# A division on VectorE queued one planner slot earlier, and the transposes of its result placed behind a mask product

## Chip, cores, metric

One Trainium2 chip (trn2), one NeuronCore of it. The metric is the device time of one launch in microseconds (us). Engines are called as the profile calls them: PE (TensorE; PEld is its weight load), DVE (VectorE), ACT (ScalarE), POOL (GpSimd), SP (SyncE, which issues most DMAs). PSUM is the memory that PE writes its products to; a "bank" is one 128 x 512 float32 tile of it.

## What is computed

Two transformer layers over x of shape (4, 512, 256), float32 throughout:

```python
x = x + L0_attn(layernorm(x))   # 16 heads of 16, causal softmax, output projection
x = x + L0_ffn(layernorm(x))    # per output unit: softmax over 8 experts, top 2, weighted expert outputs
x = x + L1_attn(layernorm(x))   # 16 query heads of 128, 4 kv heads, over groups of 4 rows
x = x + L1_ffn(layernorm(x))    # gate/up/down with 4-bit weights, gelu
```

The change lies in the first line, where the attention's mixed values are divided by the sums of the powers:

```python
att = jax.nn.softmax(jnp.where(causal, -1e9, q @ k.T / 4), axis=-1)
out = att @ v                       # (b, h, q, d)
return out.transpose(0, 2, 1, 3).reshape(b, s, d) @ w_out.T
```

## The kernel before

**Tiling.** Rows lie as 4 blocks j of 4 sequences s with 128 rows each. The first layer's attention runs over 44 batches n (line 810). A batch is a block, a sequence and some of the four groups g of four heads: 4 groups at a time in block 0 (4 batches, n = 0 to 3), 2 in block 1 (n = 4 to 11), 1 in blocks 2 and 3 (n = 12 to 27 and 28 to 43). So 16 times, once for each (j, s), the groups of a sequence are complete and are divided.

**One batch.** The program writes out the order of PE, DVE and POOL by hand (manual_schedule, line 69): these engines run in the order of the Python text. ACT's and SP's orders in this part are left to the scheduler, which is told to put the batch's own work first (high_priority). For batch n the text issues:

1. greatest(n+1): PE scores s1 into four banks of the pool l0_sc, which has five (L631).
2. shift(n): PE transposes batch n's row maxima (mxT, L660), DVE subtracts them from the queries (qk, L663).
3. mask(n+1): PE adds the causal mask (L644), DVE takes the row maxima of the four tiles (mx, L650).
4. a **first slot** (fill, line 826).
5. mixed(n-1): PE multiplies powers with values (av, L715), ACT copies the result to SBUF (avs, L723).
6. powers(n): PE scores again, transposed (s, L679, four banks of l0_sc), ACT takes exponentials (pt, L688), POOL masks them (L698).
7. a **second slot** (line 834), ahead of which divided() of a completed sequence is put at the head of the streams.

**Slots.** fill() counts the variable slot up by one, gives PE and DVE a budget of some us, and lets the streams (generators) emit pieces in order of the list while budget is left. A piece names its engine, a planned cost and a least number of slots since the stream's last piece. Pieces are the next block's projections (qk_ps L529, v_ps L551), bias folds (a product L244 and two DVE additions to rw or ew, L250), layernorms, the router's and the experts' products (lg_ps, eo, L226) and the DVE work that turns router logits into weights (L363 to L420). The left-over of the budget decides which piece comes in which slot, so that a piece moved by one slot moves later pieces too. Slots 1, 3, 5, ... are first slots as long as no extra fill is made between blocks.

**The two banks.** Every product that a slot's pieces make goes into a tile of the pool dn, which has two banks (line 97). A bank is free again when ACT (copy) or DVE has read it. The tile of the transposed mixed values (av_T), that of the transposed divided values (oq_T) and all pieces' tiles share these two banks.

**divided(j, s)** (lines 727 to 773), three steps: four PE transposes of avs into av_T (L733); on DVE a reciprocal of the sums (rden, L739) and a product (oq, L740), which are av_T's readers; two PE transposes of oq into oq_T (L748), which ACT copies to aT (L751). After the last sequence of a block, the output projection (o, L760) and the addition to x (L770) follow, and a stream for the next layernorm is added. Each step waits one slot after the one before: with av_T in the second slot of batch n, the division comes in the first slot of batch n+1, behind mask(n+2) on DVE, and oq_T in the second slot of n+1, behind powers(n+1) on PE and, in ACT's order, behind its four exponentials.

**After it.** From about 432 us on the second layer's attention runs (its weights wqkv are loaded then), with what is left of the router and expert products between its own; then the second FFN, nearly PE alone. The stage tile (one buffer, lines 581 and 539) holds projected queries and keys until eight DMAs have moved them to qk.

Of the kernel before, what the change touches and what calls it, by code (L numbers as in the profile page):

```python
# [32 lines left out]
def tile_transformer(  # L33
# [75 lines left out]
    slot = 0  # L109

    def need(engine, cost, gap=0, cond=None):
        return engine, cost, gap, cond
# [25 lines left out]
    left = {"PE": 0.0, "DVE": 0.0}  # L138
# [117 lines left out]
    def hidden_pieces(b):  # L256

        out = []
        done = (4 * b - 5, 1)
        last = b == NBLK - 1  # L260
        yield from norm_pieces(b, b1, b2, out, cond=lambda: b < 2 or done in halves)
        xT = b2.tile([P, 2, 512], F32, tag="xT", name=f"xT{b}")
        for hc in range(2):
            yield need("PE", 0.5, 0 if hc else 1 + last)
            ps = transposed(out[0], hc, ps_dn, "dn", f"xT_ps{b}_{hc}")
            ps = ps.rearrange("p t q -> p (t q)")
            if hc:
                nc.scalar.activation(xT[:, hc, :], ps, AF.Identity, bias=last_16)
            else:
                nc.scalar.copy(xT[:, hc, :], ps)  # L270
        normed.clear()
        xTs[b] = xT
# [160 lines left out]
    with ExitStack() as l0:  # L433
# [293 lines left out]
        def divided(j, s):  # L727

            yield need("PE", 0.5, 1)
            avs = avs_of.pop((j, s))  # L730
            ps = ps_dn.tile([P, NH0, 32], F32, tag="dn", name=f"av_T{j}_{s}")
            for g in range(4):
                nc.tensor.transpose(  # L733
                    ps[:, 4 * g : 4 * g + 4].rearrange("p h d -> p (h d)"), avs[:, g], ident
                )
            rden = a2.tile([P, NH0], F32, tag="rden", name=f"rden_{j}_{s}")
            oq = a1.tile([P, NH0, 16], F32, tag="oq", name=f"oq_{j}_{s}")
            yield need("DVE", 0.7, 1)
            nc.vector.reciprocal(rden, ps[:, :, 16])  # L739
            nc.vector.tensor_tensor(  # L740
                oq, ps[:, :, 0:16], rden.unsqueeze(2).to_broadcast([P, NH0, 16]), ALU.mult
            )
            yield need("PE", 0.3, 1)
            if not s:
                aTs[j] = a1.tile([P, 2, 16, NS, 8], F32, tag="aT", name=f"aT{j}")
            ps = ps_dn.tile([P, 2, P], F32, tag="dn", name=f"oq_T{j}_{s}")
            for k in range(2):
                nc.tensor.transpose(  # L748
                    ps[:, k], oq[:, 8 * k : 8 * k + 8].rearrange("p h d -> p (h d)"), ident
                )  # L750
            nc.scalar.copy(aTs[j][:, :, :, s, :], ps.rearrange("p k (g b) -> p k g b", b=8))  # L751
            if s < NS - 1:
                return

            for t in (0, 2):
                yield need("PE", 1.75, 1 if j or not t else 0)
                ps = ps_dn.tile([P, 2, HID], F32, tag="dn", name=f"o0_{j}_{t}")
                for i in range(2):
                    for k in range(2):
                        nc.tensor.matmul(  # L760
                            ps[:, i],
                            lhsT=aTs[j][:, k, 4 * (t + i) : 4 * (t + i) + 4].rearrange(
                                "p g s b -> p (g s b)"
                            ),
                            rhs=wo[:, k, :], start=k == 0, stop=k == 1,
                        )
                if j:
                    yield need("DVE", 0.7, 1)
                both = xres[:, 4 * j + t : 4 * j + t + 2, :]
                nc.vector.tensor_tensor(both, both, ps, ALU.add)  # L770
            fold_at = streams.index(fold) if fold in streams else len(streams) - 4
            streams.insert(fold_at if j else 0, Stream(hidden_pieces(j)))
# [37 lines left out]
        for n in range(NBT):  # L810
# [21 lines left out]
            if n and batches[n - 1][2][-1] == 3:  # L832
                streams.insert(0, Stream(divided(*batches[n - 1][:2])))
# [11 lines left out]
        mixed(NBT - 1)  # L845
        streams.insert(0, Stream(norm_pieces(0, b1, b2, normed_first)))
        last = Stream(divided(*batches[NBT - 1][:2]))
        streams.insert(0, last)
        while last.next is not None:
# [435 lines left out]
```

## Time and profile before

| | us |
|---|---|
| median of 3 runs | 1226.32 (1224.99 to 1227.24) |
| the profiled execution | 1226.09 |
| its span, first to last instruction | 1224.3 |
| PE busy in the span | 1170.2 (96%) |
| DVE busy | 805.4 (66%) |
| ACT busy | 483.7 (40%) |
| POOL busy | 101.4 (8%) |

How to read it: on the page "busy" is the time in which an engine ran an instruction; PEclk is the clock that PE was granted, 1 for full. In a list of waits, "PE fold L244 <- ACT stage L533: 4.1, 4, 2.1" says that PE's product for the tile fold stood idle for 4.1 us in 4 places, 2.1 at most, until ACT's copy to the tile stage ended. In a timeline a row has start, duration, engine, line, operation, tiles written and read, and in brackets the idle time before it with what ended it. A table of stretches has, for each, its length and the busy time of each engine.

### The profile page before, as it was taken

What the parts mean: (1) busy time and instruction counts of PE and PEld (TensorE: products, weight loads), DVE (VectorE), ACT (ScalarE), POOL (GpSimd) and SP (SyncE); (2) the same over time, 40 slices, a digit from 0 to 9 for tenths busy, and PEclk for the clock granted to TensorE, in tenths of its full rate; (3) what the DMA queues carried; (4) which work ended last, traced back from release to release, by engine and by line L of the source; (5) the groups of instructions that cost most, each with busy time, mean ns of one, the idle gap of its engine ahead of it and who ended that gap; (6) DMA issues with size and microseconds to landing.
All of it is one profiled execution on the core that took longest, in us unless ns stands there. A gap on an engine that the chain in (4) does not pass through costs nothing.

```text
span 1224.3 us, 18602 instructions
## 1 busy us (share of the span) xinstructions
PE 1170.2 (96%) x7178; PEld 672.7 (55%) x7178; DVE 805.4 (66%) x1783; ACT 483.7 (40%) x1099; POOL 101.4 (8%) x152
## 2 busy tenths in 40 slices
PE   7879999999989998999999999999999999999998
PEld 4545545455545543555555555656645456475487
DVE  5546658898878848726872886688599963734710
ACT  1423444564545544434443444355344331312300
POOL 7312101111111100000000000000000000000000
PEclk9999999999999999999999999999999999999999
DMA  7321010000000050000000001012020000000000
GB/s 209 68 55 18 2 32 5 1 2 1 1 1 2 1 172 1 1 1 1 1 1 1 1 1 35 16 46 44 1 52 17 1 1 18 0 1 18 0 1 34
DMA packets 21240, 26.46 MB, mean 22 GB/s; under 512 B 5128, under 2 KB 14600, under 8 KB 21152
## 3 DMA queue, kind: packets, MB, share of 16 engines
q1 hardware_dynamic: 20480, 24.10, 7.4%
q10 hardware_dynamic: 672, 1.18, 0.4%
q8 instruction: 56, 0.92, 0.3%
q14 instruction: 32, 0.26, 0.1%
HBM read 18.97 MB, written 2.10 MB: 17 GB/s over the span
## 4 chain that ended last, share of the span: by engine, by line
PE 80%; DVE 13%; ACT 3%; issue 1%; DMA 1%; POOL 1%; SPq 1%; ACTq 0%; DVEq 0%; POOLq 0%
PE qk_ps L965 10%; PE y L1212 9%; PE o L1056 9%; PE g L893 8%; PE u L893 8%; PE lg_ps L226 8%; PE eo L226 7%; PE s L631 5%; DVE mx L650 3%; PE s L679 2%; PE v_ps L947 2%; PE av L715 2%; PE qk_ps L529 2%; PE a L1036 1%; PE s L978 1%
## 5 line engine op out<-in xcount | busy, mean ns | idle before, releaser
L965 PE MATMUL qk_ps<-xT,wqkv 128*128 128x512 f32 x320 | 148.8, 599 | 1.4 <-ACT qT L969 0.8
L226 PE MATMUL lg_ps<-rw,xT 128*128 128x512 f32 x256 | 129.1, 628 | 6.9 <-ACT part L315 2.9
L226 PE MATMUL eo<-ew,xT 128*128 128x512 f32 x256 | 122.1, 600 | 4.9 <-ACT part L315 2.4
L1056 PE MATMUL o<-wpj,oT 128*128 128x256 f32 x512 | 119.6, 382 | 0.0
L1212 PE MATMUL y<-wd,it 128*128 128x256 f32 x512 | 111.8, 379 | 0.0
L1056 PEld LDWEIGHTS o<-wpj,oT 128*128 128x128 f32 x512 | 95.8, 190 | 27.8 <-issue 14.8
L1212 PEld LDWEIGHTS y<-wd,it 128*128 128x128 f32 x512 | 97.0, 190 | 15.0 <-issue 2.2
L650 DVE TENSOR_REDUCE mx<-s 128x1 f32<-128x384 f32 (+3 forms) x176 | 100.3, 631 | 1.3 <-PE s L644 1.3
L965 PEld LDWEIGHTS qk_ps<-xT,wqkv 128*128 128x128 f32 x320 | 59.1, 190 | 70.8 <-issue 57.5
L688 ACT ACTIVATE pt<-s 128x512 f32<-128x512 f32 (+1 forms) x176 | 83.6, 560 | 18.6 <-PE s L679 18.6
L893 PE MATMUL g<-xT,wgu 128*128 128x512 f32 x192 | 90.4, 593 | 0.0
L893 PE MATMUL u<-xT,wgu 128*128 128x512 f32 x192 | 90.2, 592 | 0.0
L315 ACT ACTIVATE part<-eo,c 128x256 f32<-128x256 f32 x128 | 53.8, 473 | 85.9 <-PE eo L226 82.4
L698 POOL TENSOR_SCALAR_AFFINE_SELECT pt<-pt 128x256 f32<-128x256 f32 (+2 forms) x88 | 56.0, 640 | 309.2 <-ACT pt L688 308.5
L226 PEld LDWEIGHTS lg_ps<-rw,xT 128*128 128x128 f32 x256 | 48.1, 199 | 53.5 <-issue 39.5
L1190 ACT ACTIVATE th<-sq 128x512 f32<-128x512 f32 x64 | 40.3, 630 | 87.6 <-DVE sq L1189 87.6
L631 PE MATMUL s<-qk 32*128 32x128 f32 (+3 forms) x512 | 71.0, 485 | 2.5 <-ACT pt L688 2.3
L226 PEld LDWEIGHTS eo<-ew,xT 128*128 128x128 f32 x256 | 46.2, 190 | 48.8 <-issue 36.8
L214 DVE TENSOR_TENSOR xres<-xres,y 128x256 f32<-128x256 f32 x16 | 6.7, 421 | 92.5 <-PE y L1212 92.5
L342 DVE TENSOR_TENSOR part<-part 128x512 f32<-128x512 f32 x32 | 22.1, 691 | 67.1 <-ACT part L315 67.1
L289 ACT COPY lg<-lg_ps 128x512 f32<-128x512 f32 x64 | 37.7, 589 | 71.3 <-PE lg_ps L226 71.1
L177 POOL TENSOR_TENSOR ln_rs<-rs_v,minus_half 128x4 f32<-128x4 f32 x16 | 17.8, 1112 | 555.6 <-DVE rs_v L176 305.3
(233 smaller groups left out, 1788.9 us busy)
## 6 DMA issues: line engine op xcount, KB each, us to landing
qk<-stage SPq DMA_DIRECT2D x56, 64.0 KB, 2.4
wqkv<-in_w_qkv SPq DMA_DIRECT2D x8, 320.0 KB, 6.4
rw<-in_router_w SPq DMA_DIRECT2D x8, 256.0 KB, 7.7
ew<-in_expert_w SPq DMA_DIRECT2D x8, 256.0 KB, 4.3
wpj<-in_w_proj SPq DMA_DIRECT2D x1, 2048.0 KB
out<-xres SPq DMA_DIRECT2D x4, 512.0 KB, 2.6
xres<-in_x SPq DMA_DIRECT2D x3, 512.0 KB, 9.0
dq_wgu<-in_gate_w SPq DMA_DIRECT2D x8, 128.0 KB, 2.4
```

The lines of the kernel that those rows point to most:

```text
L226: nc.tensor.matmul(ps, lhsT=xT[:, hc, (g % 4) * P : (g % 4 + 1) * P], rhs=w[:, hc, 2 * pair : 2 * pair + 2, :].rearrange("p e o -> p (e o) ...
L289: nc.scalar.copy(lg[:, 2 * pair : 2 * pair + 2, :].rearrange("p e o -> p (e o)"), ps)
L315: nc.scalar.mul(part[:, e % 4], ps[:, i], c[:, e : e + 1])
L631: nc.tensor.matmul(tiles[h][:, b * nk : (b + 1) * nk].rearrange("p (c k) -> p c k", k=P), lhsT=queries(j, g)[r, s], rhs=qk[r, g, : j + 1, ...
L650: nc.vector.tensor_reduce(maxes[n % 2][:, h, gs[0] : gs[0] + nb], ps[:, : nb * nk].rearrange("p (b k) -> p b k", b=nb), AX.X, ALU.max,)
L688: nc.scalar.activation(pt[:, i, : nb * nk], tiles[2 * pair + i][:, : nb * nk], AF.Exp, scale=0.25)
L698: nc.gpsimd.affine_select(out=last, in_=last, compare_op=ALU.is_ge, fill=0.0, base=0, pattern=pattern, channel_multiplier=-1,)
L893: nc.tensor.matmul(ps, lhsT=wgu[:, w, half, jj, par * P : (par + 1) * P], rhs=xT[:, half, :], start=half == 0, stop=half == 1,)
L965: nc.tensor.matmul(ps, lhsT=wqkv[:, hc, kv, h, :], rhs=xT[:, hc, :], start=hc == 0, stop=hc == 1,)
L1056: nc.tensor.matmul(ys[t // 2][:, t % 2], lhsT=state["o"][:, h, t * P : (t + 1) * P], rhs=wpj[:, HPK * kv + h, :], start=kv == 0 and h == 0 ...
L1190: nc.scalar.activation(th, sq, AF.Tanh, scale=0.7978845608028654)
L1212: nc.tensor.matmul(ps, lhsT=it[:, c // 2, c % 2, t * P : (t + 1) * P], rhs=wd[:, c // 2, c % 2, :], start=c == 0, stop=c == 2 * NJ - 1,)
```

## The change

The division is no longer a piece of its own: the reciprocal and the product are issued to DVE directly after the four transposes, in the same slot, and their 0.7 us are taken off DVE's budget. The transposes of the divided values are still at least one slot later, but only in a slot with an odd number, which is a first slot, behind mask().

```diff
         yield need("PE", 0.5, 1)
         avs = avs_of.pop((j, s))
...
-            yield need("DVE", 0.7, 1)
+            left["DVE"] -= 0.7
             nc.vector.reciprocal(rden, ps[:, :, 16])
             nc.vector.tensor_tensor(
                 oq, ps[:, :, 0:16], rden.unsqueeze(2).to_broadcast([P, NH0, 16]), ALU.mult
             )
-            yield need("PE", 0.3, 1)
+
+            yield need("PE", 0.3, 1, cond=lambda: slot % 2)
```

In the built programs both kernels hold the same instructions; their order differs from the first division on. The steps of divided() for a sequence then stand so: av_T and the division in the second slot of batch n, oq_T in the first slot of batch n+1 (for one sequence, j = 3 and s = 1, three batches later, since no budget is left in the first slots between).

## Prediction, made before the changed kernel ran

> **What bounds the kernel now.** I read the page first: PE is busy 96% of the span, so the end is set by PE's work and by the 54 us in which PE is idle. Then the table of stretches, cut where the batches of block 0 (to 105.1), block 1's first five (to 144.7), the rest of the first attention (to 432) and the start of the second layer (to 482) end:
>
> ```profile
> core 0: us, PE busy (x) PEld busy (x) DVE busy (x) ACT busy (x) POOL busy (x), PEclk, DMA share, GB/s
> 45.00:105.10 60.10, 47.65 (x473) 29.18 (x473) 31.72 (x58) 19.38 (x38) 13.94 (x17) 0.94 0.25 55
> 105.10:144.70 39.60, 35.53 (x405) 22.47 (x404) 24.30 (x54) 15.95 (x32) 8.36 (x12) 0.96 0.01 1
> 144.70:432.00 287.30, 273.90 (x2730) 149.41 (x2730) 231.51 (x562) 147.44 (x399) 43.45 (x71) 0.97 0.03 5
> 432.00:482.00 50.00, 42.71 (x129) 18.26 (x127) 31.00 (x90) 22.68 (x64) 0.00 (x0) 0.97 0.32 106
> ```
>
> Sixteen of PE's idle us lie in the first 100 us of this, at 0.94 and 0.96 of the clock. DVE is half busy there, 81% later. What PE waits for between 45 and 145, by the list of waits:
>
> ```profile
> PE fold L244 <- ACT stage L533: 4.1, 4, 2.1
> PE qk_ps L529 <- ACT aT L751: 3.6, 2, 2.0
> PE x_ps L202 <- ACT xT L566: 2.3, 2, 1.7
> PE v_ps L551 <- ACT aT L751: 1.7, 1, 1.7
> PE fold L244 <- ACT va L557: 1.3, 2, 0.7
> ```
>
> None of these products reads what it waits for: a fold needs neither stage nor va. They wait for a dn bank. The timeline of batch 2 shows why two banks act as one:
>
> ```profile
> 57.04 0.66 PE L733 MATMUL av_T<-ident,avs 128*128 128x128 f32 x4
> 57.18 2.06 ACT L688 ACTIVATE pt<-s 128x512 f32<-128x512 f32 x4 [0.53 <-PE s L679]
> 57.53 0.38 PE L748 MATMUL oq_T<-ident,oq 128*128 128x128 f32 x2
> ...
> 59.11 0.40 ACT L751 COPY aT<-oq_T 128x256 f32<-128x256 f32 x1
> 59.56 1.99 PE L551 MATMUL v_ps<-wp,xT 128*128 128x256 f32 x8 [1.65 <-ACT aT L751]
> ...
> 62.23 0.38 PE L244 MATMUL fold<-rows 128*128 128x512 bf16 x1 [0.67 <-ACT va L557]
> ...
> 66.78 0.38 PE L244 MATMUL fold<-rows 128*128 128x512 bf16 x1 [0.67 <-ACT va L557]
> 66.98 0.24 DVE L739 RECIPROCAL rden<-av_T 128x16 f32<-128x16 f32 x1
> ```
>
> av_T is written at 57.04, and its reader on DVE comes at 66.98, behind four row maxima: for ten us one bank is out of use. The other goes to oq_T, whose copy stands behind four exponentials (57.18 to 59.24), so v_ps idles 1.65, and each product after it waits for the copy of the one before.
>
> **Part 1: the division moves up.** DVE runs it right behind av_T. In this stretch DVE is idle then (6.33 us ahead of its addition at 62.65), so its 0.67 us (0.24 and 0.42) cost PE nothing, and the bank is free about 0.9 us after av_T, while PE runs the 1.82 us product in the other bank. In the built order that product takes the bank of the last fold, already added, and only the fold after it takes av_T's bank. On DVE the shift is queued behind the division; it waits for mxT, 4 us after av_T. **Part 2: oq_T moves behind the mask**, where ACT has no exponentials ahead of it: its 0.4 us copy is done before the next bank is needed.
>
> **Block 0**, at full clock, PE start to start: av and s 2.12 (54.92 to 57.04), av_T 0.49, a 512-wide product 1.82 (45.41 to 47.23), fold 0.31, s1 with mxT and mask 1.57 (62.54 to 64.11), oq_T 0.27. A new batch is 2.12+0.49+1.82+0.31+1.57+0.27+1.82+0.31 = 8.7. Batches now begin (av) at 54.92, 67.09, 80.92, 96.01 and 105.11: 12.2, 13.8, 15.1 and 9.1. New: 8.7, 8.7, then 9.7 (the stage tile stays taken until its eight DMAs have landed; the copy at 79.98 freed it for the next only at 88.97, 9.0 after the product's end, and the new order reaches that point earlier: I charge 1.0), then 7.6 (2.12+1.82+0.31+1.57+1.82; the first half of o stands in front of s1, which now runs 1.1 longer because it waits for exponentials). That is 34.7 for 50.2: 15.5. Ahead of 54.92 the two waits for xT copies (0.68 each) shrink to one bank wait of about 0.35, and oq_T's 0.27 comes in while xn is awaited anyway: 1.2. Together **-16.7**. Bounds: -10 (the named waits only, with half of the clock loss) to -18 (all idle and clock loss of the stretch).
>
> In these sums goes the clock. Nine times between 45 and 482 PE ran at half the clock for 3.4 us (from 72.5, 89.6, 130.6, 171.5, 198.8, 226.1, 294.4, 345.6 and 478.7: granted 0.50 or 0.51); each time PE had been busy only 21 to 67% of the 3.4 us before. A half-speed stretch costs up to 1.7 us of work. I count those at 72.5, 89.6, 130.6 and 478.7 as gone with the idle time ahead of them. The Trainium skill's page "TensorE: Matmul & The Clock Gate" (HAM oscillation) has another rule: no PE-idle gaps over some 3.4 us. The longest gap ahead of any of the nine is 2.9 us, so this trace shows it with less; by the rule these gaps would not be the cause, and the four stretches would stay (a rival below).
>
> **Block 1 to 144.7.** Now 10.96, 7.70, 13.24 and 7.70. New, from the same rows: 2.12+0.59+2.24 (s1 still behind exponentials, as from 107.81 to 110.05 now)+0.60+0.27+1.0 (xT_ps, no bank wait)+0.2+1.82 = 8.8; 2.12+1.82+1.57+1.0 (x_ps)+0.25+1.82 = 8.6; 2.12+0.49+1.82+1.57+0.27+1.82 = 8.1; 2.12+1.82+1.57+1.82 = 7.3. 32.8 for 39.6, with the 1.65 and 0.68 at 128.62 and 129.96 and their slow stretch gone: **-6.8** (bounds -3 to -7).
>
> **144.7 to 432.** The wait of 2.73 at 171.81 is for av_T's bank too; in the new order its place is taken by o, which waits for a stage copy behind exponentials (some 2.2): -0.5. Pieces change slots; slots with no product on PE cost up to 1.2 (224.83 and 292.19: s1 waits for exponentials; 197.31: av waits for the shift). Before, six first and three second slots of batches 16 to 42 are empty; after, six and four. Batch 33 gains cover for the 2.06 at 344.50. DVE runs late here: the division comes ahead of the maxima in eight batches, 0.67 each, 5.4 if all reached PE. I take **-0.5** in all, bounds +6 and -8 (nearest rows: the 12 us of named PE waits here).
>
> **432 to 482.** Now DVE idles 15.0 us until 457.33, then is late: softmax waits behind router weights, and PE idles 1.73 and 2.87 (472.31, 478.89), with a slow stretch. In the new order lg_ps8_3 comes ahead of the second layer's projections, so DVE does that group's weights in its idle time. **-4**, between 0 and -6.3 (1.73+2.87+1.7). After 482 PE is 99% busy in both: 0.
>
> **Sum.** 16.7+6.8+0.5+4 = 28.0 off the profiled execution's own 1226.1 (span 1224.3 and 1.8 around it, unchanged): 1198.1; the median of the runs shown is 0.2 above that execution: **1198.3**.
>
> **Rivals.** (a) *The gain is given back in blocks 2 and 3.* For it: DVE 81% busy, empty slots as many as before. Against: DVE still waits 47.7 us for mxT there. Eight divisions at 0.67+0.6 of new wait give +10 there: 1209. (b) *The slow stretches stay*, 4 x 1.7: 1205. Against: each follows an idle stretch. (c) *Slower: DVE stands at the reciprocal.* Everything behind it, the next shift and maxima, waits for av_T, which stands behind s on PE. Behind mxT, DVE needs 2.2 to 3.2 us for shift and maxima, and PE 3.4 (mask 0.5, product 1.8, av 1.1) until s needs the maxima's banks; so it decides where division and the slot's other pieces end more than about 0.5 us after mxT. If each of 16 divisions made an idle of 1.2 and a slow stretch (1.7), 46 less 28: 1245. Against: in block 0 DVE has 3 us to spare, and in batch 16 DVE comes to that place at 201.4, with av_T done at 201.3. (d) *Nothing:* av_T's bank is not what PE waits for, or another stage wait replaces it: 1226. Against: the division's place in the timeline.
>
> **Chances.** Forecast (1191 to 1207) 0.62; (a) 0.14; (b) 0.08; still faster, outside these 0.06; (d) 0.04; (c) 0.06. Faster 0.90, same 0.04, slower 0.06; 0.2% is about what this measurement can tell from none. The range takes the bounds of the terms: 1190 to 1216.
>
> **What would show it.** Right: av starts of block 0 about 8.7 apart; no wait of qk_ps or v_ps for aT; the reciprocal within 0.3 us of av_T's end; 105.1 becoming about 88, 144.7 about 121; no half clock before 110. Wrong: PE waiting for the shift or maxima in batches with a division; folds still waiting; the lead at 121 not kept at 410.

## The result, and the profile after

The changed kernel takes **1184.12 us** in the median (1182.2 to 1186.06, 4 runs) where the kernel before takes 1226.78 (1224.99 to 1227.38, 4 runs): a ratio of 0.9655, with a 95% interval of 0.963 to 0.9679. It is faster, as forecast, by 42.7 us where 28.0 were forecast, and lies below the range. The profiled execution took 1185.96 (span 1184.2), 40.1 less than the profiled one of before; the sums below are made against these two.

The table of stretches, with the first two cut where the same work ends (av of batch 5, av of batch 9) and the other two 32 us earlier than those of before. Columns: stretch, its length, busy time and instructions of PE, PEld, DVE, ACT, POOL, granted clock, DMA share, GB/s.

```profile
45.00:88.60 43.60, 42.44 (x493) 27.67 (x485) 31.39 (x59) 19.71 (x39) 13.96 (x17) 1.00 0.36 80
88.60:123.50 34.90, 33.88 (x405) 22.03 (x404) 21.91 (x52) 16.05 (x32) 8.34 (x12) 1.00 0.01 2
123.50:400.00 276.50, 266.30 (x2726) 144.49 (x2725) 236.36 (x566) 148.74 (x401) 48.19 (x71) 0.98 0.03 5
400.00:450.00 50.00, 45.51 (x147) 20.97 (x148) 37.60 (x114) 25.21 (x68) 2.01 (x2) 1.00 0.32 106
```

PE's idle time ahead of batch 9 has gone from 16.5 us to 2.2, and the clock there is full. In the list of PE's waits between 45 and 123.5 (total, times, longest) no fold waits for va, no v_ps for aT, and one qk_ps still waits for aT:

```profile
PE xT_ps L202 <- DVE xn L186: 0.5, 2, 0.3
PE qk_ps L529 <- ACT aT L753: 0.5, 1, 0.5
...
PE fold L244 <- ACT stage L533: 0.2, 1, 0.2
```

The timeline of batch 2 shows the new order at work (start, duration, engine, line, operation):

```profile
56.25 0.66 PE L733 MATMUL av_T<-ident,avs 128*128 128x128 f32 x4
...
56.74 1.89 PE L551 MATMUL v_ps<-wp,xT 128*128 128x256 f32 x8
56.94 0.26 DVE L740 RECIPROCAL rden<-av_T 128x16 f32<-128x16 f32 x1 [1.42 <-PE av_T L733]
57.23 0.42 DVE L741 TENSOR_TENSOR oq<-av_T,rden 128x256 f32<-128x256 f32 x1
...
60.46 0.38 PE L750 MATMUL oq_T<-ident,oq 128*128 128x128 f32 x2
60.67 1.89 PE L551 MATMUL v_ps<-wp,xT 128*128 128x256 f32 x8
...
60.88 0.37 ACT L753 COPY aT<-oq_T 128x256 f32<-128x256 f32 x1 [1.62 <-PE oq_T L750]
```

av_T's reader comes 0.03 us after av_T's end instead of 9.3 us, and the copy of oq_T finds ACT idle. All four divisions of block 0 start within 0.1 us of av_T's end; of the twelve later ones five start 1.0 to 2.0 us after it. v_ps follows with no bracket: it did not wait.

**Where the 40.1 us come from.** Cut by work (starts of av in batches 5, 9, 12, 28, 43, and the start of the eleventh group of scores of the second layer), the stretches of before and after are: 105.1 and 88.6 (16.5 less), 39.6 and 34.9 (4.7), 30.5 and 26.4 (4.1), 122.9 and 122.3 (0.6), 121.7 and 115.5 (6.2), 351.6 and 342.5 (9.1), and from there to the end 452.9 and 454.0 (1.1 more). 21.2 of them lie ahead of batch 9, where the prediction had 23.5; the rest had been put at 4.5 and is 18.9.

### The profile page after: what moved, and what is told of

Its sections match the earlier page's. It is cut to its first block, busy times and chain, and to the rows that moved or that the text cites. A ratio compares the mean times of both kernels' runs of the same rounds, so it can differ in the third digit from the quotient of the medians.

```text
span 1184.2 us, 18603 instructions
## 1 busy us (share of the span) xinstructions
PE 1153.4 (97%) x7178; PEld 666.0 (56%) x7178; DVE 807.9 (68%) x1783; ACT 485.2 (41%) x1099; POOL 106.4 (9%) x152
## 4 chain that ended last, share of the span: by engine, by line
PE 82%; DVE 11%; ACT 2%; issue 2%; POOL 1%; DMA 1%; SPq 0%; ACTq 0%; DVEq 0%; POOLq 0%
PE qk_ps L967 11%; PE o L1058 10%; PE y L1214 9%; PE g L895 9%; PE u L895 9%; PE lg_ps L226 8%; PE eo L226 8%; PE s L631 4%; PE s L679 3%; DVE mx L650 3%; PE av L715 2%; PE v_ps L949 2%; PE qk_ps L529 2%; PE a L1038 1%; PE s L980 1%
## 5 line engine op out<-in xcount | busy, mean ns | idle before, releaser
L226 PE MATMUL lg_ps<-rw,xT 128*128 128x512 f32 x256 | 123.6, 607 | 3.9 <-ACT xT L934 1.6
L967 PEld LDWEIGHTS qk_ps<-xT,wqkv 128*128 128x128 f32 x320 | 59.4, 190 | 68.7 <-issue 59.6
L698 POOL TENSOR_SCALAR_AFFINE_SELECT pt<-pt 128x256 f32<-128x256 f32 (+2 forms) x88 | 60.7, 696 | 266.5 <-ACT pt L688 265.8
L631 PE MATMUL s<-qk 32*128 32x128 f32 (+3 forms) x512 | 62.2, 465 | 1.2 <-ACT pt L688 0.9
L1193 DVE SCALAR_TENSOR_TENSOR th<-th,g 128x512 f32<-128x512 f32 x63 | 43.2, 686 | 29.2 <-ACT th L1192 29.2
```

The lines of the kernel that those rows point to most:

```text
L226: nc.tensor.matmul(ps, lhsT=xT[:, hc, (g % 4) * P : (g % 4 + 1) * P], rhs=w[:, hc, 2 * pair : 2 * pair + 2, :].rearrange("p e o -> p (e o) ...
L631: nc.tensor.matmul(tiles[h][:, b * nk : (b + 1) * nk].rearrange("p (c k) -> p c k", k=P), lhsT=queries(j, g)[r, s], rhs=qk[r, g, : j + 1, ...
L698: nc.gpsimd.affine_select(out=last, in_=last, compare_op=ALU.is_ge, fill=0.0, base=0, pattern=pattern, channel_multiplier=-1,)
L967: nc.tensor.matmul(ps, lhsT=wqkv[:, hc, kv, h, :], rhs=xT[:, hc, :], start=hc == 0, stop=hc == 1,)
L1193: nc.vector.scalar_tensor_tensor(th, th, 1.0, gp, ALU.add, ALU.mult)
```

## The experiments

Thirteen more kernels were run. The first four split the change by place and by part.

**The change in blocks 0 and 1 alone, and in blocks 2 and 3 alone.** The edit, for the first (the second has `j > 1`):

```diff
-            left["DVE"] -= 0.7
+            if j < 2:
+                left["DVE"] -= 0.7
+            else:
+                yield need("DVE", 0.7, 1)
...
-            yield need("PE", 0.3, 1, cond=lambda: slot % 2)
+            yield need("PE", 0.3, 1, cond=lambda: slot % 2 or not (j < 2))
```

> The change is made for blocks 0 and 1 alone; in blocks 2 and 3 the division and its transposes stand as before. The pieces of the slots stay almost where the changed kernel has them. Theory S (the lead won after block 1 comes from the pieces having moved to other slots, which leaves fewer waits of the scores s1 for ACT's exponentials): within 4 us of the changed kernel, 1181 to 1188. Theory D (it comes from the division itself being earlier in blocks 2 and 3): the 11 us won between 144.7 and 419.9 are lost, about 1195. Both: the batches of block 0 about 8.8 us apart, as with the change.

> The change is made for blocks 2 and 3 alone. Both theories: block 0 and 1 as before, so that the 21 us won there are missing. Theory D: 11 us are still won between blocks 2 and the end of the first attention, about 1216 or less. Theory S: the pieces stand in the slots nearly as before, so next to nothing is won there, 1222 to 1230.

Measured: 1187.58 (ratio 0.968, 0.9653 to 0.9707), as theory S expected (3.5 from the changed kernel), and 1220.57 (0.9942, 0.9925 to 0.9959), between what the two theories expected. The kernel before took 1226.84 beside them. The change in the first two blocks brings nearly all the gain. But with the change in them alone, the stretch from batch 28 to 43, where no division has moved, takes 116.4 instead of 121.7, and the second layer's start 341.9 instead of 351.6: something that is not the division's place travels with it.

**The division alone**, with the transposes two slots behind av_T as before, and **the change without the slot condition** (1 in place of the 2):

```diff
-            yield need("PE", 0.3, 1, cond=lambda: slot % 2)
+            yield need("PE", 0.3, 2)
```

> The division is queued with the transposes as in the change, but its own transposes stay two slots later, behind the next scores and in ACT's order behind four exponentials. Theory of the two banks: the bank of the mixed values' transposes is free early, so the waits of folds go (0.67 each and the 2.06), but the products behind the divided values' transposes still wait for its copy at first hand (1.65 to 1.98 each, three times); block 0 ends near 94 where it ended at 105.1 before and at 88.6 with the change. Rival: only the transposes' place matters, then block 0 ends as before, near 105. Total by the first 1188 to 1200, by the rival 1215 or more.

> The condition on the slot's number is left out; the order is the changed kernel's up to batch 37 of 44, then pieces fall into other slots, and the second layer begins with the router product of group 8 placed late, as before the change. If that place makes the 8 us that the changed kernel wins between 420 and 770 us, the lead shrinks there: 1189 to 1193. If that stretch is won by something else (more DVE time left over), it stays within 3 us of 1184.

Measured: 1185.56 (0.9663, 0.9637 to 0.9688) and 1190.02 (0.97, 0.9672 to 0.9728). The first is faster than expected (block 0 ends at 90.6, not near 94): the early division brings nearly all; the transposes' place is worth 2.0 in block 0 (batch 5 at 90.6 for 88.6) and no more than 1.4 in all. The second lies where it was expected if the place of lg_ps8_3 makes the loss: it is 4.5 us ahead at batch 43 (383.2 for 387.7) and loses it and more by the eleventh scores (351.4 for 342.5). In these four orders, in that of before and in the change's, one thing goes with that stretch: where the router product lg_ps8_3 stands. Ahead of the second layer's first projections (v1_ps0) the stretch takes 339.7 to 342.5 (three kernels), ten rows behind them 351.4 to 355.4 (three kernels).

**That product's place by itself.** One number brings it forward in the kernel before, without moving any division, and in the kernel without the condition:

```diff
         while last.next is not None:
-            fill(PE=2.0, DVE=2.6)
+            fill(PE=2.2, DVE=2.6)
```

> The kernel before with one number changed: the budget of the slots that finish the last divided sequence (fill behind mixed(NBT - 1)) is 2.2 instead of 2.0 for PE. No division is moved; what it does in the order is to bring the router product lg_ps8_3 ahead of the second layer's first projections (v1_ps0), as the change does. Theory Q: this place alone is a term of its own: in the four kernels measured so far with the late place or the early one, the way from the last batch's av to the eleventh group of scores takes 351.5 (before), 355.4 (change in blocks 2 and 3 alone), 351.4 (no slot condition) with the late place and 342.5 (after), 341.9 (change in blocks 0 and 1 alone), 339.7 (division alone) with the early place. So about 9 us less: 1216 to 1220. Theory P (the prediction's term, 4 us, at most 6.3): 1220.5 to 1223. Theory R (the early place helps only when the first layer has ended earlier, since what waits in the second layer is paced by something else): 1225 to 1228.

> The change without its slot condition, and the same budget of 2.2 in those last slots, so that lg_ps8_3 comes early again. Without the condition the last batch began 4.5 us earlier than in the changed kernel (383.2 for 387.7) and the late router product then lost it, 1190.0 in all. Theory Q: with the early place the 4.5 us stay, and the loss of about 9 goes: 1179 to 1183, under the changed kernel's 1184.1. Theory P: about 4 less than 1190, 1184 to 1187. Theory R: 1188 to 1191.

Measured: 1215.83 (0.9929, 0.9902 to 0.9955) and 1181.69 (0.964, 0.9617 to 0.9662), with 339.6 and 339.4 for the stretch. Theory Q holds (1225.06 was the median of before beside them): it is a term of its own, of 8 to 9 us by the medians and 12 by the stretch. The second kernel is the fastest measured with the reference's outputs, by 2.4 us, though its interval overlaps the change's. The longest waits of PE from 420 to 520, in the kernel before:

```profile
PE lg_ps L226 <- ACT part L315: 2.9, 1, 2.9
PE eo L226 <- ACT part L315: 2.4, 2, 1.7
PE eo L226 <- ACT xT L932: 1.4, 1, 1.4
PE v_ps L947 <- ACT xT L932: 1.0, 1, 1.0
...
```

and with the product brought forward, in the same window:

```profile
PE lg_ps L226 <- ACT xT L932: 1.0, 1, 1.0
PE eo L226 <- ACT part L315: 0.7, 1, 0.7
...
```

From batch 43 to the end PE idles 16.4 us before (804.4 less 788.0 busy) and 8.7 with the product forward (793.6 less 785.0); one half-clock window less makes 1.7 of the other 3.1.

**The sums on ACT.** ACT runs eight Relu sums (spare, L406) per router group, which wait for DVE's steps. Both kernels without them:

```diff
-            nc.vector.memset(sums[:, NE : NE + 1], 0.0)
+            nc.vector.memset(sums, 0.0)
...
-                defer(sum_up)
```

> The kernel before without the eight sums per router group on ACT (Relu with accum_out; the sums are set to zero instead, so the output of the first FFN is not the reference's). In blocks 2 and 3 ACT runs these sums ahead of the exponentials in its order, and the sums wait for DVE. Only the difference to the changed kernel without the same sums matters. Theory A (in blocks 2 and 3 the division's late place is paid because DVE runs late, the sums wait for DVE, and the exponentials stand behind the sums): both kernels get faster, this one by more, 1195 to 1215 and the difference to the other shrinks from 42.7 to 28 to 33. Theory B (the bank that the transposed mixed values hold, and nothing on ACT, sets it): the difference stays at 39 to 45.

> The changed kernel without the eight sums per router group on ACT (the sums are set to zero, so the output of the first FFN is not the reference's). Theory A: 1165 to 1182, 28 to 33 under the kernel before without them. Theory B: 39 to 45 under it.

Measured: 1201.91 (0.9801, 0.9763 to 0.9838) and 1174.43 (0.9587, 0.9562 to 0.9613): the difference shrinks to 27.5, just under the 28 to 33 of theory A, but mostly not where it said. PE's and DVE's orders stay as they were through the first layer's attention. The difference from batch 12 to 43 falls from 6.9 to 4.3 us (in block 3 alone from 6.2 to 1.7); most of the shrinking is at the second layer's start (9.1 to 0.5), where without sums the late product no longer hurts. What the sums do in block 3 is seen in batch 33 of the kernel before:

```profile
331.92 1.17 PE L679 MATMUL s<-qk 32*128 32x128 f32 x32
...
334.18 0.42 DVE L416 SCALAR_TENSOR_TENSOR owing<-lg,owing 128x256 f32<-128x256 f32 x1
...
334.69 0.42 ACT L406 ACTIVATE spare<-owing 128x256 bf16<-128x256 f32 x1 [2.36 <-DVE owing L416]
335.01 0.19 ACT L406 ACTIVATION_READ_ACCUMULATOR spare<-owing 128x1 f32 x1
335.10 1.07 ACT L688 ACTIVATE pt<-s 128x512 f32<-128x512 f32 x2
```

The scores begin at 331.92, their exponentials only at 335.10: in ACT's order a sum stands ahead, and it waits 2.36 us for DVE. In the same batch of the changed kernel no sum stands there:

```profile
304.44 1.94 PE L679 MATMUL s<-qk 32*128 32x128 f32 x32
304.58 0.27 ACT L723 COPY avs<-av 128x128 f32<-128x128 f32 x1 [0.54 <-PE av L715]
...
306.27 2.06 ACT L688 ACTIVATE pt<-s 128x512 f32<-128x512 f32 x4 [1.43 <-PE s L679]
```

Over block 3 the exponentials begin more than 2 us after the scores in 11 of 16 batches before (sums stand ahead of them in nine), and in 4 after (in three). The next batch's s1 needs the banks that they read. Its 128 products of block 3 show it in the groups by line and shape (busy, mean ns of one), before and after:

```profile
L631 PE MATMUL s<-qk 32*128 32x512 f32 x128 | 31.7, 668 | 1.2 <-ACT pt L688 1.2
```

```profile
L631 PE MATMUL s<-qk 32*128 32x512 f32 x128 | 23.4, 640 | 0.2 <-ACT pt L688 0.2
```

The same instructions have 8.3 us less of "busy", and hardly any of it had stood in the idle column: a group whose parts wait one by one looks like long rows. From its first row to its last in each batch, s1 of block 3 takes 32.9 us in all before and 23.6 after; without the sums 24.7 and 20.3, so about half of the difference hangs on the sums. (4.8 of the 9.3 lie in the stretch from 28 to 43; the s1 of batches 28 to 30 stands ahead of it.)

**The sums two slots later**, meant to take the wait away in the changed kernel:

```diff
-                defer(sum_up)
-                yield need("DVE", 0.95, cond=lambda: len(deferred) < 4)
+                defer(sum_up, 2)
+                yield need("DVE", 0.95, cond=lambda: len(deferred) < 6)
...
-            yield need("DVE", 0.3, 1)
+            yield need("DVE", 0.3, 1, cond=lambda: not deferred)
```

> The changed kernel with the eight sums per router group on ACT issued two slots after their inputs' piece instead of one (up to 6 of them deferred instead of 4; the last step waits until none is deferred), and PE's budget in the last slots at 2.8, which keeps the router product lg_ps8_3 ahead of the second layer's projections. The outputs are the reference's. Theory A (in block 3 exponentials start late behind sums that wait for DVE): the first exponential starts over 2 us after the batch's scores in 11 of 16 batches before the change and in 4 after it; with sums that wait for nothing in 0 to 2, and the first layer ends 3 to 7 earlier: 1176 to 1182. Theory N (the sums cost ACT's time wherever they stand): 1183 to 1188.

Measured: 1196.8 (0.977, 0.9744 to 0.9795): a miss for both theories. The exponentials still begin over 2 us late in 5 batches of block 3 (sums stand ahead of them in all five), and the second layer's start takes 351.2 with the product in front, 347.8 without its two half-clock windows. So the product's early place is not enough for a short start in every order. Moving a piece moves all later ones: the edit did not take one thing away, and tells nothing about the sums alone.

**The bank by itself.** In the kernel before, av_T gets a bank of its own; the scores lose their fifth for it, so the base has four too. Against that base no instruction changes its place on PE, DVE or POOL; ACT's order, the scheduler's, differs in four places.

```diff
-        ps_sc = l0.enter_context(tc.tile_pool(name="l0_sc", bufs=5, space=PSUM))
+        ps_sc = l0.enter_context(tc.tile_pool(name="l0_sc", bufs=4, space=PSUM))
+        ps_av = l0.enter_context(tc.tile_pool(name="l0_av", bufs=1, space=PSUM))
...
-            ps = ps_dn.tile([P, NH0, 32], F32, tag="dn", name=f"av_T{j}_{s}")
+            ps = ps_av.tile([P, NH0, 32], F32, tag="avT", name=f"av_T{j}_{s}")
```

> The kernel before with four banks for the scores instead of five, nothing else; it is the base for the next kernel, which needs a bank. The first score product of a batch loses its spare bank and waits for the exponentials or maxima of the batch before: 1230 to 1260 (44 batches by 0.1 to 0.8).

> The kernel with four score banks, and the tile of the transposed mixed values in a bank of its own instead of one of the two that all pieces share. The order of every engine and the late place of the division are as before. Bank theory (the early division pays because the bank is free early, in block 0 above all): against the kernel with four score banks alone, the stretch from 45 to the end of block 0 shrinks by 10 to 15, the whole by 14 to 24. Order theory (it pays by what DVE or ACT run in another order): the stretch shrinks by less than 4, the whole by less than 8.

Measured: 1237.68 (1.0103, 1.0069 to 1.0138) and 1219.09 (0.9955, 0.9939 to 0.997), 18.6 apart. Batch 5 comes at 108.0 with four score banks and at 91.7 with the bank of its own: 16.3, a little over the 10 to 15 expected (3.4 of it are two half-clock windows), with the division still behind the maxima. PE's longest waits of block 0, with four score banks alone:

```profile
PE qk_ps L529 <- ACT aT L751: 3.7, 2, 2.0
PE fold L244 <- ACT stage L533: 3.7, 4, 1.6
PE v_ps L551 <- ACT aT L751: 1.7, 1, 1.7
...
```

and with the bank of its own:

```profile
PE fold L244 <- ACT stage L534: 0.4, 1, 0.4
PE x_ps L202 <- DVE xn L186: 0.3, 1, 0.3
...
```

The bank theory is shown for block 0, the prediction's largest term.

**Place and slots, two by two.** The last two kernels part the division's place from the planner's reckoning. In the first the two DVE instructions stand right behind av_T, but the empty piece stays, so PE's order is that of before (ACT's, which the scheduler makes, differs in 50 of 1099 places):

```diff
-            yield need("DVE", 0.7, 1)
             nc.vector.reciprocal(rden, ps[:, :, 16])
...
+            yield need("DVE", 0.7, 1)
             yield need("PE", 0.3, 1)
```

In the second the planner reckons as in the run with the division alone, whose PE order it has, and the two instructions are put into a function (divide) that fill() calls at the start of the next slot:

```diff
         slot += 1
+        while divisions:
+            divisions.pop(0)()
...
+            divisions.append(divide)
```

> The division directly behind the transposes, as in the change, while the planner still reckons with a division piece one slot later; so every slot holds the same pieces as before the change, PE's order is that of before word for word, and only the two DVE instructions have moved. Theory T (two terms: the bank, and where the planner puts the later pieces): block 0 ends at 89 to 92 and block 1's fifth batch starts at 124 to 126; block 3 (av of batch 28 to av of batch 43) stays near the 121.7 of before, since the exponentials stand behind the same sums, and the late lg_ps8_3 keeps the second layer's start at 350 to 355 (av of batch 43 to the eleventh scores): 1196 to 1203. Theory S (the division's place is all): 1183 to 1188, with 113 to 117 in block 3 and 340 to 343 at the second layer's start.

> The counterpart: the planner reckons as in the run with the early division alone, and PE's order is that run's word for word, but the two DVE instructions are issued at the start of the next slot, behind the maxima, as before the change. Theory T: block 0 ends at 104 to 107 as before, block 3 takes 113 to 117 and the second layer's start 340 to 343: 1208 to 1214. Theory S: 1222 to 1228.

Measured: 1210.09 (0.9849, 0.9814 to 0.9884) and 1208.02 (0.9842, 0.9806 to 0.9878). Theory S is out: the first kernel misses its range by over 20 us, the second by 14. Theory T holds for the second at the edge of its range; the first is 7 us slower than it said. With the division alone (1185.56) the table is full. Stretches are cut as above, in us of the profiled executions, without the half-clock loss, which has a row of its own (half of each 3.41 us window at half clock):

| stretch | before | other slots, late place | old slots, early place | both (division alone) | the change |
|---|---|---|---|---|---|
| to batch 5 | 101.7 | 101.6 | 92.0 | 90.6 | 88.6 |
| 5 to 12 | 66.7 | 63.2 | 60.7 | 58.7 | 59.6 |
| 12 to 28 | 117.8 | 120.1 | 120.2 | 120.9 | 118.8 |
| 28 to 43 | 120.0 | 117.5 | 121.5 | 113.7 | 115.5 |
| 43 to the eleventh scores | 349.9 | 338.3 | 351.4 | 339.7 | 342.5 |
| from there | 452.9 | 454.0 | 452.9 | 454.0 | 454.0 |
| half-clock loss | 15.3 | 13.6 | 11.9 | 6.8 | 5.1 |
| span | 1224.3 | 1208.3 | 1210.7 | 1184.4 | 1184.2 |

The place alone is worth 16.9 us of the medians, the slots alone 18.9, both together 41.4 (1226.94 less 1185.56): 5.6 come only with both (10.3 in the profiled executions), mostly from block 3 (113.7) and from the clock. In block 3 the late exponentials go with the slots: they begin over 2 us after the scores in 11 of 16 batches with the old slots and the early place, in 5 with the other slots and the late place and in 4 with both; s1 there takes 32.9, 26.9 and 23.7 us. Up to batch 12 the place gives 15.7, from there it costs 5.4 with the old slots. Part of that are waits of PE (its list from batch 12 to 43, with the old slots and the early place):

```profile
PE av L715 <- DVE qk L663: 4.9, 6, 2.1
PE oq_T L748 <- ACT stage L533: 2.2, 1, 2.2
```

In the kernel before, between the same batches, the first of these is 3.4 in 6 places and the second is not there. Theory T left this cost out when it expected 1196 to 1203 for the early place; it had 113 to 117 in block 3 for the other slots, which took 117.5.

## Why the prediction was wrong in size, step by step

**Block 0, -16.7: right.** 16.5 measured. The batches begin at 54.13, 62.71, 71.27, 80.89 and 88.64: 8.6, 8.6, 9.6 and 7.7 apart, for 8.7, 8.7, 9.7 and 7.6. The bank of av_T was the main cause, shown by the kernel with a bank of its own and by that with the early place and PE's old order (batch 5 at 92.0); the new place of oq_T is worth 2.0 of it. In the profiled execution no half clock falls before 110, so the two windows at 72.5 and 89.6 went with the idle time, and rival (b) fell.

**Block 1, -6.8: somewhat too much.** 4.7 measured; the batches take 10.3, 8.9, 8.2 and 7.5 for 8.8, 8.6, 8.1 and 7.3. Most of the miss is the first one: the eight xT transposes wait for xn twice, and the next product starts at 97.07, 2.5 after the first of them (94.58), where 1.2 had been put. One reading is off by a little: the 1.57 for s1, mxT and mask runs from a product's start to a weight load's (62.54 to 64.11); from product to product it is 1.68 (62.54 to 64.22).

**144.7 to 432, -0.5 with bounds of +6 and -8: the step that failed.** 11.0 measured from batch 9 to batch 43. It failed in three ways. The bounds came from "the 12 us of named PE waits here", but PE's idle time gave only 4.8 of the 11.0: the rest lies inside rows counted as busy (s1 of block 3: 9.3 us less from first row to last) and in the clock (five half-clock windows before, three after: 3.4). The effect of the moved slots was judged by counting empty slots (six and three before, six and four after), which says nothing of what stands ahead of the exponentials on ACT. The built order would have told: batches with sums ahead of their exponentials in ACT's order could be counted in it (nine of block 3 before, five after, by the traces). And 4.1 us lie in batches 9 to 11, which are still block 1: the prediction ended the bank's gain at 144.7, but for the wait at 171.81. There the early place alone gives 3.3 and av_T's own bank 2.9, half-clock loss taken off. The wait at 171.81 did go as foreseen: o stands 2.2 us for stage in its place.

**432 to 482, -4, at most 6.3: right in cause, too small.** The change gains 9.1 up to the eleventh scores and loses 1.1 behind them. lg_ps8_3's place was named, and moved alone it is worth 9.2 us of the medians (1225.06 to 1215.83). The term took two waits of the list (1.73 and 2.87) for all of it; the list has more, and with the product moved alone PE's idle time up to the end fell by 7.7, 2.5 of it behind 482, where the prediction had put nothing. In the changed kernel it fell by 3.9; the other 4.1 of the 8.0 lie in rows counted as busy, 1.7 of them by the clock.

**The clock: counted too low.** Nine half-clock windows before, three after in the profiled executions: 10.2 us, where four windows (6.8) had been counted in the sums.

**The range.** The bounds of the four terms add up to 7.0 and 39.3 us off, which is 1187 to 1219, not 1190 to 1216; the 1184.12 measured lies below both.

**Rivals.** (a), the gain given back in blocks 2 and 3, is real where the division alone moves in the old slots (5.4 from batch 12 on, 3.8 of it in blocks 2 and 3). It does not come with the whole change in nearly the old slots: with the change in blocks 2 and 3 alone the stretches from 12 to 28 and from 28 to 43 take 116.6 and 116.2, half-clock loss taken off, for 117.8 and 120.0. Whether oq_T's place or the few moved pieces make that difference was not tested. (c), DVE standing at the reciprocal, does occur (1.42 us ahead of it in batch 2) but hardly reaches PE: in the changed kernel from 123.5 to 400 PE waits for the shift 1.0 us in 6 places, 0.3 at most. (d) fell.

What stays open: why the pieces happen to fall better in block 3. The runs show that they do, with and without the moved division, and that about half of what s1 gains hangs on the sums; the other half is not settled.

## What to carry to other kernels

A tile that shares a small pool holds its bank until its reader's turn comes on the reader's engine: look for the tile whose reader comes latest, and price the wait of everything that then goes through the remaining bank. When an edit changes what a planner reckons, the pieces that it moves elsewhere may be worth as much as the edit: test it in two kernels, one with the old plan and the new place, one with the reverse. Bounds taken from the list of waits are too narrow where groups of short products wait part by part; compare the length of the same group in undisturbed batches.

## What the runs showed of the hardware

**A half clock can follow rows that show no idle.** At 138.6 in the changed kernel the granted clock halves for one window although PE's rows fill the 3.41 us before (stretches with length, busy times and clock, then PE's timeline):

```profile
135.19:138.60 3.41, 3.41 (x15) 1.80 (x15) 1.97 (x4) 2.76 (x6) 1.32 (x2) 1.00 0.00 0
138.60:142.00 3.40, 3.40 (x12) 1.07 (x14) 3.37 (x11) 0.31 (x1) 0.00 (x0) 0.50 0.02 5
```

```profile
135.28 2.67 PE L631 MATMUL s<-qk 32*128 32x384 f32 x8
```

The same eight products take 0.93 us at 127.97, so some 1.7 us of the row are waiting. The window at 247.84 of the changed kernel and one in each of three other kernels follow 3.41 us in which PE's rows fill 94 to 95%, with no gap over 0.2 us. That waits inside rows bring the clock down is read from such stretches; no run tests it by itself. The Trainium skill's page "TensorE: Matmul & The Clock Gate" (HAM oscillation) gives the rule "no PE-idle gaps >~3.4µs". This trace does not bear it out as a limit: here no gap is shown at all, and ahead of the nine windows of before the longest is 2.9 us.

**Half-clock windows lie on a grid.** In the profiles of fourteen kernels the starts of such windows (71 intervals) are whole multiples of 3.4135 us apart, within 0.05 us: in the kernel before 5, 12, 12, 8, 8, 20, 15, 39 and 218 of them. So, it seems, the same idle stretch can cost 1.7 us in one run and nothing in another, by where it lies on the grid. In the kernel before and in that with lg_ps8_3 forward, PE runs block 0 in the same order and idles 21.1 and 20.9 us up to batch 5, which begins at 105.1 and 103.3, with two such windows and with one.
